# Three small reorderings in a fused attention and ternary-expert kernel on one core: two weight signs behind the first tanh, one value product behind a down product, one block's sums copied out of PSUM by ScalarE

## The chip, the core and the metric

The kernel runs on one NeuronCore of a Trainium2 chip. The core has five engines that run their own instruction streams and meet at semaphores: TensorE (PE in the profile) multiplies matrices into the accumulator memory PSUM; VectorE (DVE) and ScalarE (ACT) read and write PSUM and the on-chip memory SBUF; GpSimd (POOL) works on SBUF; SyncE (SP) issues the transfers to and from HBM. Weight loads of TensorE have a row of their own, PEld. Each engine takes its instructions in program order, so an instruction that waits holds up everything behind it on its engine.

The metric is the device time of one launch in microseconds, all data starting and ending in HBM. Of the kernel before, three timed executions are shown; their median is 1167.89 us.

## The reference, cut to what matters

The input is 2 x 2048 rows of 512 numbers. An attention over 64 fixed latent keys and a gated expert network follow one another, each with a normalisation before and after and a residual sum.

```python
# attention: 16 heads of 32, 64 latent keys per head, the four largest logits are kept
Q = (h @ Wq.T + bq)...;  V = (h @ Wv.T + bv)...
attn_logits = einsum('bhtd,lhd->bhtl', Q, latent) / sqrt(32)
topk_logits, topk_idx = top_k(attn_logits, 4)
weighted = einsum('bhtk,bhtkd->bhtd', softmax(topk_logits), latent_h[..., topk_idx])
attn_output = (weighted + V) @ Wo.T + bo

# expert network, 512 -> 2048 -> 512, weights rounded to -1, 0, 1 times a scale
wu, wg, wd = ternary_quant(W_up), ternary_quant(W_gate), ternary_quant(W_down)
hidden = silu(x @ wu.T) * (x @ wg.T)
ffn = hidden @ wd.T

x = x + layernorm(attention(layernorm(x)))
x = x + layernorm(ffn(layernorm(x)))
```

`ternary_quant` takes the mean of |W| as the scale, divides, rounds and clips to -1, 0 or 1.

## The kernel before, in words

The 4096 rows are worked in eight blocks (`NB`) of 512 rows; a block is four tiles of 128 rows. A block's expert network is sixteen chunks `e` of 128 hidden columns. The order of all instructions on all engines is the program's order: a manual schedule is in force and nothing is moved by a planner.

**First part.** A written list of steps, `FIRST_STEPS` (line 35 on), does block 0's attention, starts block 1's, and turns part of the expert weights into ternary form. A weight tile is made in three steps: `sum_abs` (ScalarE) for the scale, `rounded` (line 228, GpSimd, in place) and `sign` (line 232, ScalarE, raw to `tern`). The last four steps on the list are `rdd0 rdd1 sgd0 sgd1`: the rounding and the sign of the first two tiles of the down weights (`tern_d`). The tiles that the list does not make are made during block 0's experts by `rest(e, place)` (line 872) from the table `REST` (line 865): for the chunk that an entry names, the rounding is issued behind `tanh`, the sign behind `high`.

**The loop over chunks.** For each chunk e of a block (line 995 on), the order is: `up("u", e)`, eight matmuls into the PSUM buffer `pu`; `tanh` (ScalarE, L693); in block 0 `rest(e, "tanh")`; `silu` (VectorE, L696), which frees `pu`; `up("g", e)` into `pg`; `gate` (VectorE, L701), which frees `pg`; `high` (ScalarE, L712), a rounded copy of the product; in block 0 `rest(e, "high")`; `down(e - 1)`, the eight matmuls of the chunk before into the four accumulators `acc` (L727); `low` (VectorE, L717), what the rounded copy leaves over. `pu` and `pg` exist once each (`ps_up`, one buffer per tag), so the next chunk's up product waits for this chunk's silu, and its gate product for this chunk's gate. The four `acc` tiles (`ps_acc`, four buffers) are shared by all blocks.

**The next block's attention** lies between these steps. `pieces` (line 882) gives a table: `put(e, k, f, ...)` places a step of the next block in chunk e at one of four places, in the order of the code: 3 behind the up product, 0 behind tanh, 1 behind the gate product, 2 behind the down product. For block 1, the value product `v` (four matmul instructions of two passes, L435) and its attention part `y` (two more, L452, and the ScalarE copy `attnT`, L442) of column chunk 0 stand at place 1 of chunk 5, those of column chunk 1 at place 1 of chunk 7. They write one of the two PSUM buffers of `ps_at`, which the logit products `l` (L362) also use; those are emptied by ScalarE into `w` (L370). VectorE does the top four (`m`, `r`, lines 376 and 383), `n` the weights, `z` (L415) a transpose that goes through HBM into `wT`.

**The end of a block.** Its last down product is issued in chunk 0 of the next block. Behind it, `y_stats` (VectorE, L249 and L250) takes mean and variance of each `acc` tile and `y_rstd` (GpSimd, L256 to L259) the inverse deviation. In chunk 1, behind silu and ahead of the gate product, `y_out` (line 765) applies the norm to each of the four tiles: `Norm.apply` (line 275, L276, VectorE, out of PSUM into an SBUF `row` buffer, of which there are four), a GpSimd addition to the residual (L769) and the output transfer by SyncE (L771). The block's own first down product into `acc` is issued in chunk 1 and needs the four tiles free. The last block has no next attention in it.

Of the kernel before, what the change touches and what calls it, by code (L numbers as in the profile page):

```python
# [42 lines left out]
y3 scg rdg6 o3_2 yc3 rdg4 o2_3 sgg6 o3_3 ost2 rdg0 sgg4 o1_3 ost3 ors2 sgg0 o0_3 ost1 ors3 nq1  # L43
sd4 onm2 ost0 ors1 oap2 onm3 oap3 ors0 oad2 oad3 rdg2 onm0 fst2 oap0 nq2 nqc1 oad0 frs2 sgg2
onm1 fst3 oap1 fap2 frs3 oad1 fst1 nq3 nqc2 fap3 frs1 fst0 fap1 frs0 ftr3 fap0 nqc3 fhi3 ftr0
flo3 fhi0 flo0 ftr1 fhi1 ftr2 flo1 fhi2 flo2 totd scd rdd0 rdd1 sgd0 sgd1
"""

LAST_O = ((0, 3), (1, 3), (2, 3), (3, 3))
# [9 lines left out]
def latent_attention_ternary_glu(  # L59
# [15 lines left out]
    nc = tc.nc  # L75
    NT, D = x_in.shape
    E = wuT.shape[1]
    DC = D // P
# [3 lines left out]
    NB = NT // TB  # L82
# [49 lines left out]
    def load_x(b):  # L132
        x_tiles[b] = []
        for t in range(TT):
            xt = work.tile([P, D], F32, tag="x", name=f"x_{b}_{t}", bufs=2 * TT)
            r = b * TB + t * P
            nc.sync.dma_start(out=xt, in_=x_in[r : r + P, :])
            x_tiles[b].append(xt)
# [4 lines left out]
    def load_normed(b):  # L143
        for t in range(TT):
            xt = work.tile([P, D], F32, tag="xa", name=f"xa_{b}_{t}", bufs=TT)
            r = b * TB + t * P
            nc.sync.dma_start(out=xt, in_=x_in[r : r + P, :])
            normed[b, t] = xt
# [79 lines left out]
    def rounded(n, i):  # L228
        w = raw[n, i]
        nc.gpsimd.tensor_scalar(w, w, inverses[n], MAGIC, ALU.mult, ALU.add)  # L230

    def sign(n, i):
        j = i if n != "d" or i < 6 else 6 + (i - 6) // 2
        if (n, j) not in tern:
            tern[n, j] = wpool.tile([P, CH], F32R, tag="chunk", name=f"tern_{n}_{j}", bufs=6 * DC)
        q = tern[n, j] if j == i and i < 6 or n != "d" else tern[n, j][:, (i % 2) * D : (i % 2 + 1) * D]
        nc.scalar.activation(q, raw[n, i], AF.Sign, bias=minus_magic)  # L237
# [42 lines left out]
    def row(name):  # L280
        return work.tile([P, D], F32, tag="row", name=name, bufs=4)
# [250 lines left out]
    class FirstAttention(SecondAttention):  # L532
# [79 lines left out]
        def y_copy(self, c):  # L612
            nc.scalar.activation(
                self.attnT[:, c, :], self.pv.pop(c), AF.Identity, bias=bqv_sb[:, 1, c : c + 1]
            )
# [57 lines left out]
    class Experts:  # L673
# [58 lines left out]
        def y_stats(self, t):  # L732
            self.norm.stats(t, self.acc[t])

        def y_rstd(self, lo, hi):
            self.norm.rstd(lo, hi, out_scale)

# [26 lines left out]

        def y_out(self, t, engine=nc.gpsimd):
            x = x_tiles[self.b][t]
            y = row(f"y_{self.b}_{t}")
            self.norm.apply(y, self.acc[t], t)
            engine.tensor_tensor(x, x, y, ALU.add)  # L769
            r = self.b * TB + t * P  # L770
            nc.sync.dma_start(out=out[r : r + P, :], in_=x)  # L771
# [4 lines left out]
    A = FirstAttention(0)  # L776
# [83 lines left out]
    for step in FIRST_STEPS.split():  # L860
# [2 lines left out]


    REST = (
        [(1, "d", 2)] + [(2 + i // 2, "u", 2 * i + 1) for i in range(DC)]
        + [(4 + i // 2, "g", 2 * i + 1) for i in range(DC)]
        + [(6, "d", 3), (7, "d", 4), (8, "d", 5)]
        + [(9 + i // 2, "d", 6 + i) for i in range(DC)]
# [1 line left out]

    def rest(e, place):
        for chunk, n, i in REST:
            if chunk == e and place == "tanh":
                rounded(n, i)
            elif chunk == e and place == "high":
                sign(n, i)
# [4 lines left out]
    def pieces(A, after):  # L882

        at = {(e, k): [] for e in range(EC) for k in range(4)}

        def put(e, k, f, *args):
            at[e, k].append(lambda: f(*args))

        if A.b > 1:
            if A.b == 2:  # L890
                put(0, 0, A.a_apply, 0)
                put(0, 0, A.a_apply, 1)
                put(0, 1, A.a_trans, 0)
                put(0, 1, A.a_trans, 1)
                put(0, 1, A.a_apply, 2)
                put(0, 1, A.a_apply, 3)
                put(0, 2, A.a_trans, 2)
                put(0, 2, A.a_trans, 3)
            put(1, 0, A.q, 0)
            put(2, 0, A.q, 1)  # L900
            put(4, 0, A.q, 2)
            put(6, 0, A.q, 3)
        put(1, 1, A.l, 0)
        put(2, 2, A.l, 1)
        for i in range(8):
            put(2 + i, 0, A.m, i)
            put(2 + i, 2, A.r, i)
            put(3 + i, 3, A.e, i)
            put(3 + i, 1, A.n, i)
            put(3 + i, 1, A.z, i)  # L910
        for c in range(2):
            if A.b > 1:
                put(5 + 2 * c, 0, A.v, c, gate_psum)
                put(5 + 2 * c, 0, A.y, c)
            put(5 + 2 * c, 0, A.l, c + 2)
            if A.b == 1:
                put(5 + 2 * c, 1, A.v, c)
                put(5 + 2 * c, 1, A.y, c)
        for c in range(2, DC):
            put(5 + 2 * c, 1, A.v, c)  # L920
            put(5 + 2 * c, 1, A.y, c)
        if after is not None and after.b == 2:
            put(14, 2, after.a_stats, 0)
            put(14, 2, after.a_stats, 1)
            put(15, 1, after.a_stats, 2)
            put(15, 1, after.a_stats, 3)
            put(15, 1, after.a_rstd, 0, 4)
        elif after is not None:
            put(10, 2, after.a_stats, 0)
            put(10, 2, after.a_stats, 1)  # L930
            put(11, 0, after.a_stats, 2)
            put(11, 0, after.a_stats, 3)
            put(11, 0, after.a_rstd, 0, TT)
            for t in range(TT):
                put(11, 1, after.a_apply, t)
            for c in range(DC):
                put(11, 2, after.a_blocks, c)
            put(15, 2, after.a_load)
        put(11, 2, A.o, 0, range(DC), gate_psum)
        put(11, 2, A.o_bias, 0)  # L940
        for t in range(1, TT):
            put(11, 2, A.o, t)
            put(11, 2, A.o_bias, t)
        put(11, 2, A.o_rstd, 0, 2)
        put(12, 1, A.o_rstd, 2, 4)
        put(12, 2, A.o_apply, 0)
        put(12, 2, A.o_apply, 1)
        put(13, 0, A.o_apply, 2)
        put(13, 0, A.o_apply, 3)
        put(13, 1, A.f_stats, 0)  # L950
        put(13, 1, A.f_stats, 1)
        put(13, 1, A.f_rstd, 0, 2)
        put(13, 2, A.f_stats, 2)
        put(13, 2, A.f_stats, 3)
        put(13, 2, A.f_rstd, 2, 4)
        put(14, 0, A.f_apply, 0)
        put(14, 0, A.f_apply, 1)
        put(14, 1, A.f_alloc)
        put(14, 1, A.f_trans, 0)
        put(14, 1, A.f_trans, 1)  # L960
        put(14, 1, A.f_apply, 2)
        put(14, 1, A.f_apply, 3)
        put(15, 0, A.f_trans, 2)
        put(15, 0, A.f_trans, 3)
        return at

    prev = None
    for b in range(NB):
        if b > 0:
            A, nxt = nxt, after  # L970
        after = None
        F = Experts(b, (A.hi, A.lo))
        at = {}
        for e in range(EC):
            if e == 4 and 0 < b < NB - 1:
                load_x(b + 1)
            if e == (12 if b == 0 else 6) and b + 2 < NB:
                load_normed(b + 2)
            if e == 4:
                after = (SecondAttention if b == 0 else Attention)(b + 2) if b + 2 < NB else None  # L980
                if b + 1 < NB:
                    later = pieces(nxt, after)
                    at.update({k: v for k, v in later.items() if k[0] >= 4})
            elif e == 0 and b + 1 < NB:
                at.update({k: v for k, v in pieces(nxt, None).items() if k[0] < 4})

            def do(k):
                for f in at.get((e, k), ()):
                    f()

            def first(place):
                if b == 0:
                    rest(e, place)

            F.up("u", e)
            do(3)
            F.tanh(e)
            first("tanh")
            do(0)
            F.silu(e)  # L1000
            if e == 1 and prev is not None:
                for t in range(TT):
                    prev.y_out(t)
            F.up("g", e)
            do(1)
            F.gate(e)
            F.high(e)
            first("high")
            if b == NB - 1 and e >= EC - 2:
                pass  # L1010
            elif e > 0:
                F.down(e - 1)
            elif prev is not None:
                prev.down(EC - 1)
            do(2)
            if e == 0 and prev is not None:
                for t in range(TT):
                    prev.y_stats(t)
                prev.y_rstd(0, TT)
            F.low(e)  # L1020
        prev = F
# [73 lines left out]
```

## Time and profile before

| | before |
|---|---|
| timed executions, median (lowest to highest) | 1167.89 us (1167.62 to 1168.21) |
| profiled execution, its own time | 1165.54 us |
| span of the profiled execution, first to last instruction | 1163.7 us |
| mean granted clock of TensorE | 0.997 |
| PE busy | 1144.5 us, 98% |
| VectorE busy | 854.1 us, 73% |
| ScalarE busy | 370.8 us, 32% |
| GpSimd busy | 174.4 us, 15% |

The span is what the trace covers; the execution's own time is 1.8 us more. In the rows of a timeline the first number is the start in us from the span's start, the second the length, then engine, line of the program, operation, tile written and tiles read with their shape; in brackets at the end stands how long the engine was idle before it and what ended that. In a line of waits the numbers are total us, how many and the longest. In a table of stretches each engine has its busy us and, in brackets, its instructions; behind them stand the granted clock, the share of DMA time and GB/s.

### The profile page before, as it was taken

What the parts mean: (1) busy time and instruction counts of PE and PEld (TensorE: products, weight loads), DVE (VectorE), ACT (ScalarE), POOL (GpSimd) and SP (SyncE); (2) the same over time, 40 slices, a digit from 0 to 9 for tenths busy, and PEclk for the clock granted to TensorE, in tenths of its full rate; (3) what the DMA queues carried; (4) which work ended last, traced back from release to release, by engine and by line L of the source; (5) the groups of instructions that cost most, each with busy time, mean ns of one, the idle gap of its engine ahead of it and who ended that gap; (6) DMA issues with size and microseconds to landing.
All of it is one profiled execution on the core that took longest, in us unless ns stands there. A gap on an engine that the chain in (4) does not pass through costs nothing.

```text
span 1163.7 us, 14548 instructions
## 1 busy us (share of the span) xinstructions
PE 1144.5 (98%) x4730; PEld 786.2 (68%) x4730; DVE 854.1 (73%) x2974; ACT 370.8 (32%) x653; POOL 174.4 (15%) x213
## 2 busy tenths in 40 slices
PE   9999999999999999999999999999999999999997
PEld 5447665776757666677757766587665866757885
DVE  6977984967967779668887688776886868847335
ACT  4984531333213332123222232122331232312222
POOL 1056001310023000320003200032001320013001
PEclk9999999999999999999999999999999999999999
DMA  9700211023212221122220231211411112100000
GB/s 348 294 0 6 68 63 47 1 88 102 64 37 64 82 91 57 34 73 82 91 82 0 73 127 56 72 34 42 138 61 55 37 63 83 64 10 10 28 1 36
DMA packets 73323, 80.38 MB, mean 69 GB/s; under 512 B 7200, under 2 KB 46368, under 8 KB 73248
## 3 DMA queue, kind: packets, MB, share of 16 engines
q1 hardware_dynamic: 73248, 79.46, 20.9%
q8 instruction: 37, 0.61, 0.2%
q14 instruction: 38, 0.31, 0.1%
HBM read 51.12 MB, written 28.31 MB: 68 GB/s over the span
## 4 chain that ended last, share of the span: by engine, by line
PE 87%; DVE 4%; DMA 3%; ACT 2%; issue 1%; POOL 1%; SPq 1%; ACTq 0%; POOLq 0%
PE acc L727 19%; PE pg L684 19%; PE pu L684 19%; PE pv L435 8%; PE po L463 8%; PE pq L348 7%; PE pv L452 2%; PE pl L362 2%; PE pt_f L286 1%; DMA raw_d<-in_wdT 1%; DMA raw_g<-in_wgT 1%; DMA bo_sb<-in_bo 1%; DVE left L388 1%; DMA raw_u<-in_wuT 1%; ACT tern_g L237 1%
## 5 line engine op out<-in xcount | busy, mean ns | idle before, releaser
L684 PE MATMUL pg<-hT_f,tern_g 128*128 128x512 f32 x512 | 211.7, 413 | 0.0
L684 PE MATMUL pu<-hT_f,tern_u 128*128 128x512 f32 x512 | 204.4, 399 | 1.5 <-DVE h L696 1.5
L727 PE MATMUL acc<-tern_d,hi 128*128 128x512 f32 x512 | 203.8, 398 | 1.7 <-DVE y L276 1.7
L727 PE MATMUL acc<-tern_d,lo 128*128 128x512 f32 x512 | 200.3, 391 | 0.1
L684 PE MATMUL pu<-lT_f,tern_u 128*128 128x512 f32 x512 | 200.2, 391 | 0.1
L684 PE MATMUL pg<-lT_f,tern_g 128*128 128x512 f32 x512 | 199.8, 390 | 0.0
L712 ACT CAST hi<-h 128x512 fp32r<-128x512 f32 x128 | 79.4, 620 | 260.0 <-DVE h L701 259.9
L693 ACT ACTIVATE h<-pu,columns 128x512 f32<-128x512 f32 x128 | 87.2, 682 | 216.4 <-PE pu L684 215.6
L701 DVE TENSOR_TENSOR h<-h,pg 128x512 f32<-128x512 f32 x128 | 86.2, 673 | 78.7 <-PE pg L684 77.9
L696 DVE SCALAR_TENSOR_TENSOR h<-h,pu 128x512 f32<-128x512 f32 x128 | 86.2, 674 | 71.2 <-ACT h L693 71.2
L717 DVE TENSOR_TENSOR lo<-h,hi 128x512 fp32r<-128x512 f32 x128 | 96.2, 752 | 35.6 <-ACT hi L712 35.6
L727 PEld LDWEIGHTS acc<-tern_d,hi 128*128 128x128 f32 x512 | 96.2, 188 | 36.2 <-issue 15.0
L684 PEld LDWEIGHTS pg<-hT_f,tern_g 128*128 128x128 f32 x512 | 96.2, 188 | 26.2 <-issue 4.1
L684 PEld LDWEIGHTS pu<-hT_f,tern_u 128*128 128x128 f32 x512 | 96.6, 189 | 24.7 <-DVE h L696 2.4
L684 PEld LDWEIGHTS pg<-lT_f,tern_g 128*128 128x128 f32 x512 | 96.3, 188 | 24.2 <-issue 5.7
L684 PEld LDWEIGHTS pu<-lT_f,tern_u 128*128 128x128 f32 x512 | 96.7, 189 | 21.5 <-issue 1.7
L727 PEld LDWEIGHTS acc<-tern_d,lo 128*128 128x128 f32 x512 | 96.4, 188 | 19.7 <-DVE lo L717 0.9
L435 PE MATMUL pv<-hT,wv 128*128 128x512 f32 x224 | 100.9, 593 | 2.2 <-ACT w L370 2.1
L388 DVE MATCH_REPLACE8 left<-m,w 128x64 f32<-128x64 f32 x512 | 100.3, 210 | 0.0
L463 PE MATMUL po<-wo,attnT 128*128 128x512 f32 x224 | 97.3, 592 | 0.0
L348 PE MATMUL pq<-hT,wq 128*128 128x512 f32 x192 | 86.3, 592 | 0.0
L463 PEld LDWEIGHTS po<-wo,attnT 128*128 128x128 f32 x224 | 42.6, 190 | 50.7 <-issue 48.5
(128 smaller groups left out, 1321.4 us busy)
## 6 DMA issues: line engine op xcount, KB each, us to landing
dz<-z SPq DMA_DIRECT2D x56, 256.0 KB, 2.0
wT<-dz SPq DMA_DIRECT2D x224, 64.0 KB, 1.9
x<-in_x SPq DMA_DIRECT2D x32, 256.0 KB, 3.5
out_x<-x SPq DMA_DIRECT2D x31, 256.0 KB, 2.0
xa<-in_x SPq DMA_DIRECT2D x24, 256.0 KB, 3.4
da<-za SPq DMA_DIRECT2D x20, 256.0 KB, 2.9
hT<-da SPq DMA_DIRECT2D x20, 256.0 KB, 5.2
raw_u<-in_wuT SPq DMA_DIRECT2D x8, 512.0 KB, 8.6
```

The lines of the kernel that those rows point to most:

```text
L348: nc.tensor.matmul(pq, lhsT=wq[:, k, c * P : (c + 1) * P], rhs=self.taken(k), start=(k == 0), stop=(k == DC - 1),)
L362: nc.tensor.matmul(pls[pr][:, t * P : (t + 1) * P], lhsT=qT[rows, t * P : (t + 1) * P], rhs=lk[rows, c, :], start=True, stop=True, tile_po ...
L388: nc.vector.match_replace(left[:, g, :], m8[:, g, :], w[:, g, :], TAKEN)
L435: nc.tensor.matmul(self.pv[c], lhsT=wv[:, k, c * P : (c + 1) * P], rhs=self.ordered(k), start=(k == 0), stop=False,)
L463: nc.tensor.matmul(self.po[t], lhsT=self.attnT[:, c, t * P : (t + 1) * P], rhs=wo[:, c, :], start=(c == 0), stop=(c == DC - 1),)
L684: nc.tensor.matmul(p, lhsT=tern[n, 2 * k + e // 8][:, (e % 8) * P : (e % 8 + 1) * P], rhs=part[:, k, :], start=(k == 0 and i == 0), stop=( ...
L693: nc.scalar.activation(self.h[e], self.pu[e], AF.Tanh, scale=half_u[0])
L696: nc.vector.scalar_tensor_tensor(self.h[e], self.h[e], 1.0, self.pu.pop(e), ALU.add, ALU.mult)
L701: nc.vector.tensor_tensor(self.h[e], self.h[e], self.pg.pop(e), ALU.mult)
L712: nc.scalar.copy(hi, self.h[e])
L717: nc.vector.tensor_tensor(lo, self.h.pop(e), self.hid[e][0].bitcast(F32), ALU.subtract)
L727: nc.tensor.matmul(self.acc[t], lhsT=part[:, t * P : (t + 1) * P], rhs=wd, start=(e == 0 and i == 0), stop=(e == EC - 1 and i == 1),)
```

## The change

It has three parts.

1. The two signs of the first down-weight tiles leave the written list. Sign 0 is issued behind the tanh of chunk 0 of block 0, sign 1 behind its `high`. Their roundings stay where they were.
2. For block 1, the value product of column chunk 0 moves from place 1 of chunk 5 (ahead of the down product) to place 2 (behind it). Column chunk 1 stays.
3. In the last block (which ends the second to last), a ScalarE copy of each `acc` tile into an SBUF row is issued ahead of the statistics of that tile. The statistics still read `acc`; the apply of `y_out` reads the copy and writes it in place. The other blocks are as before.

```diff
-flo3 fhi0 flo0 ftr1 fhi1 ftr2 flo1 fhi2 flo2 totd scd rdd0 rdd1 sgd0 sgd1
+flo3 fhi0 flo0 ftr1 fhi1 ftr2 flo1 fhi2 flo2 totd scd rdd0 rdd1
...
+        def y_copy(self, t):
+            self.y = getattr(self, "y", {})
+            self.y[t] = row(f"y_{self.b}_{t}")
+            nc.scalar.copy(self.y[t], self.acc[t])
...
         def y_out(self, t, engine=nc.gpsimd):
             x = x_tiles[self.b][t]
-            y = row(f"y_{self.b}_{t}")
-            self.norm.apply(y, self.acc[t], t)
+            if self.b == NB - 2:
+                y = self.y[t]
+                self.norm.apply(y, y, t)
+            else:
+                y = row(f"y_{self.b}_{t}")
+                self.norm.apply(y, self.acc[t], t)
             engine.tensor_tensor(x, x, y, ALU.add)
...
-        [(1, "d", 2)] + [(2 + i // 2, "u", 2 * i + 1) for i in range(DC)]
+        [(0, "d", 0), (0, "d", 1), (1, "d", 2)] + [(2 + i // 2, "u", 2 * i + 1) for i in range(DC)]
...
         for chunk, n, i in REST:
-            if chunk == e and place == "tanh":
+            if e == 0:
+
+                if chunk == 0 and i == ("tanh", "high").index(place):
+                    sign(n, i)
+            elif chunk == e and place == "tanh":
                 rounded(n, i)
...
             if A.b == 1:
-                put(5 + 2 * c, 1, A.v, c)
-                put(5 + 2 * c, 1, A.y, c)
+                put(5 + 2 * c, 2 - c, A.v, c)
+                put(5 + 2 * c, 2 - c, A.y, c)
...
                 for t in range(TT):
+                    if b == NB - 1:
+                        prev.y_copy(t)
                     prev.y_stats(t)
```

## The prediction

> **What bounds the kernel now.** I read the page's busy shares first, then the waits of TensorE, then the timeline around each long wait, then the clock by stretch. TensorE (PE) is busy 98% of the span:
>
> ```profile
> PE 1144.5 (98%) x4730; PEld 786.2 (68%) x4730; DVE 854.1 (73%) x2974; ACT 370.8 (32%) x653; POOL 174.4 (15%) x213
> PE pv L435 <- ACT w L370: 2.1, 1, 2.1
> PE acc L727 <- DVE y L276: 1.7, 1, 1.7
> PE pu L684 <- DVE h L696: 1.5, 1, 1.5
> ```
>
> The last three lines are the longest waits of PE (total, how many, longest). Each happens once and all else is under 1.1 us, so only these three places can repay moving work on other engines. The first two places, both in block 0:
>
> ```profile
> 92.08 2.25 ACT L237 ACTIVATE tern_d<-raw_d,columns 128x1024 fp32r<-128x1024 f32 x2 [2.44 <-POOL raw_d L230]
> 94.24 0.67 ACT L693 ACTIVATE h<-pu,columns 128x512 f32<-128x512 f32 x1
> 95.68 0.50 PE L684 MATMUL pu<-hT_f,tern_u 128*128 128x512 f32 x1 [1.53 <-DVE h L696]
> ...
> 123.93 2.19 ACT L237 ACTIVATE tern_g<-raw_g,columns 128x1024 fp32r<-128x1024 f32 x2
> 125.67 0.69 DVE L717 TENSOR_TENSOR lo<-h,hi 128x512 fp32r<-128x512 f32 x1
> 127.23 1.07 ACT L370 ACTIVATE w<-pl 128x512 f32<-128x512 f32 x2
> 127.87 3.70 PE L435 MATMUL pv<-hT,wv 128*128 128x512 f32 x8 [2.13 <-ACT w L370]
> ```
>
> At 92 us two signs stand ahead of the first tanh on ScalarE; expert chunk 1's up product waits behind tanh and silu. At 125 us the value product waits until ScalarE has emptied one of two PSUM buffers. The third place, start of the last block, with the clock:
>
> ```profile
> 1072.20 2.97 DVE L276 TENSOR_SCALAR y<-acc,mv_y,rs_y 128x512 f32<-128x512 f32 x4 [1.02 <-POOL rs_y L259]
> 1073.16 0.47 PE L727 MATMUL acc<-tern_d,hi 128*128 128x512 f32 x1 [1.68 <-DVE y L276]
> 1075.09 0.68 DVE L701 TENSOR_TENSOR h<-h,pg 128x512 f32<-128x512 f32 x1
> ...
> 1075.00:1077.00 2.00, 2.00 (x6) 1.49 (x5) 1.32 (x3) 0.62 (x1) 2.00 (x3) 0.52 0.59 223
> 1077.00:1079.00 2.00, 2.00 (x7) 1.54 (x7) 0.42 (x1) 0.00 (x0) 1.55 (x1) 0.63 0.46 170
> ```
>
> In the two stretches the granted clock (third number from the end) falls to 0.52 and 0.63; matmuls step at 0.425 us instead of 0.2265 (eight in 1.81 us). So this wait costs far more than 1.7 us. Last, how the two engines that share work on the rows disturb each other, in an earlier place of block 7:
>
> ```profile
> 1043.67 1.52 POOL L479 TENSOR_TENSOR x<-x,o 128x512 f32<-128x512 f32 x1 [1.75 <-DVE o L276]
> 1043.96 1.78 DVE L717 TENSOR_TENSOR lo<-h,hi 128x512 fp32r<-128x512 f32 x1
> 1045.15 1.74 POOL L479 TENSOR_TENSOR x<-x,o 128x512 f32<-128x512 f32 x1
> 1045.67 1.51 DVE L276 TENSOR_SCALAR o<-o,mv_o,rs_o 128x512 f32<-128x512 f32 x1
> ```
>
> An apply that reads SBUF takes 0.54 us alone but 1.51 beside a POOL add, ending 0.29 us after that add does; the subtraction ends 0.55 us after its add. The 28 applies that read PSUM take 0.80 us each whether POOL adds or not.
>
> **Part 1, the signs.** Nothing is removed: the same two signs of 1.15 us move, and no DMA and no POOL work goes with them. The first up product ends at 92.32, so tanh runs 92.36 to 93.03, silu (0.69) to 93.75, and the second up product may start where PE is free: its last matmul began at 93.77, plus a step, 94.00. It started at 95.68, so 1.68 is gained here. Behind the tanh on ScalarE now stand sign 0 (to 94.10), the high part (gate ends 94.89, so to 95.54) and sign 1 (to 96.60); tanh 1 waits for sign 1 instead of for PE at 95.97, and silu 1 ends 97.95, where gate 1 may begin anyway (its matmuls end 97.8). Sign 0 is needed by the first down product at about 98.95. So late next is nothing up to chunk 2. From there to 127 us the chain runs through VectorE (DVE), which is busy 4.8 to 4.9 of each 5 us from 110 on and moves up as a whole, but meets POOL's roundings, which do not move (busy without a gap from 90.93 to 110.34). In the trace two operations of DVE lost 0.37 and 0.41 there (1.06 and 1.10 against 0.69). Coming 1.7 earlier they find more roundings left; a loss is at most one rounding of 0.81 each, and a third operation may be hit. I take 1.4 us; ends 0.7 and 1.7.
>
> **Part 2, the value product.** Six matmuls and one ScalarE copy move behind the down product of chunk 4; no DMA. In the times of before: PE is free at 125.58. The down product's first matmul can go, the second needs the low part (done 126.36), so it runs from 126.42 on and ends its eight steps at 128.00. The value product's PSUM buffer is empty at 127.80: no wait. So 2.29 of standstill becomes about 0.6, worth 1.7 at this point. What is queued behind: on ScalarE the copy of the values (it waited for PE until 132.65) stood ahead of high part 5 and two signs; now high part 5 runs at 131.08 behind its gate (131.04), the signs to 133.8, then the copy to 134.44, the exponentials to 135.1, tanh 6 to 135.72 instead of 137.16. So DVE's silu 6 starts 1.44 earlier, and with it everything up to the next two copies that empty PSUM; the second value product starts at 143.65 instead of 145.09, now 0.7 behind PE where it was 0.25. What DVE and ScalarE allow, 1.44, therefore decides. Behind 150 us the trace has no PE wait to the block's end and all shifts together. I take 1.4; ends 0 (the chain of DVE does not move at all) and 1.7.
>
> **Part 3, the copies.** Four copies PSUM to SBUF are added on ScalarE. No row has this form; the nearest is the copy of attention's 128x512 PSUM tile, 0.58 to 0.59 us, 0.5 when one follows another. The rows they write were last read by the transposes that ended at 1058.8. They start behind high part 0 (ends 1067.43), are done by 1069.5, and the tanh behind them began at 1069.77, when its matmuls ended: hidden. Were that cover gone (copies of 0.8, as DVE reads PSUM), tanh 1 would end 0.9 late, still before its silu blocks PE (1073.14). The PSUM sums are free when the statistics end, 1069.79, not when the applies do, so the down product runs at 1071.33 without a wait.
>
> Late next is the gate of chunk 1, which stands on DVE behind the four applies, and whose PSUM buffer PE needs for the gate product of chunk 2, now already at 1074.95. The applies read SBUF now. Following the rows above: apply 0 runs 1072.20 to 1072.74, apply 1 to 1073.20 (the second of a pair took 0.54 beside a waiting add), add 0 then holds until 1074.34, apply 2 ends 1074.63, add 1 holds until 1075.78, apply 3 ends 1076.07, the gate 1076.68. PE starts at 1076.73: 1.78 of new wait. The low part behind it is issued at 1077.37, meets the last add (until 1078.46) and ends 1079.0; the down product's second matmul wanted it at 1078.78: 0.27 more. Sum of the loss after the change 2.05. Before: that gate product began at 1079.13 against 1074.95, a loss of 4.18. Gain 2.1. SP's output DMAs follow the adds, which end at 1078.5 as before.
>
> The low end: every apply but the first costs 1.51 and the clock falls again. Of the 4.18, 1.62 is the half clock (from 1075.23 to 1078.66 eight steps took 3.43 instead of 1.81). 2.8 + 0.3 + 1.62 = 4.7, so 0.6 lost (three applies of 1.51, each overlapping the next by 0.08, end the gate about 1.0 later than above). The high end: applies of 0.54 throughout, gate done at 1075.1, loss nearly none: 4.1 gained.
>
> Two rules of the Trainium skill bear on this part. In "SBUF — State Buffer", section "Who interferes with whom", whoever of DVE and GpSimd issues first holds the shared pair of ports for its whole instruction, and an operation that reads one tensor from PSUM is exempt. It speaks against this change, and the 1.51 and 0.80 us rows agree with it; by the rule the gain is the 2.1 of the sum, by the row of a lone apply (0.54) it would be 4.1. "TensorE: Matmul & The Clock Gate", section "Part 1: The HAM clock gate", of the Trainium skill has the clock fall after an idle window of about 3.4 us; here it fell with no gap above 1.68 us, so the measurement decides and a fall after a 1.8 us gap is not excluded, as it would be by that page.
>
> **Sum.** 1.4 + 1.4 + 2.1 = 4.9 us off the profiled 1165.54 us (span 1163.7 and 1.8 around it), 1160.6 there. The timed median is 2.35 us above that execution, for reasons the profile does not show; taken off it, 1163.0 us.
>
> **The rivals.** (A) No turn-taking: all applies run at 0.54 us because DVE keeps winning over POOL. For it: two in a row did. Against it: the third operation at 1043.96 lost. Gain 4.1 in part 3: 1161.0 us. (B) The half clock is not what part 3 saves, either because it falls again behind the new 1.8 us wait or because the timed runs of before did not have it. For it: the fall at 1075 with gaps of 1.68 and three of about 0.4. Against it: after the gaps of 1.53 and 2.13 us in block 0 the clock stayed 1.00. Without the 1.62, part 3 gives 0.5: 1164.6 us. (C) Block 0 is bound by DVE and POOL, and the two gains there come to 0.6 together instead of 2.8, as new waits of PE at about 104 to 127. For it: DVE's 97%. Against it: DVE's own start hangs on the chain that moves. 1165.2 us. (D) Slower: the new wait in front of the gate product starts a longer spell at half clock. Each us of it costs 0.47 (0.425 against 0.2265 a step). It eats the 4.9 at 10 us and is beyond 0.2% at 15 us, where the spell of before lasted 3.2; a clock that stays down for 16 us gives 1170.5 us. Nothing in block 0 speaks for it.
>
> **How the numbers follow.** 0.2%, about what a measurement of this kernel can tell from no change, is 2.3 us: below 1165.6 is faster, above 1170.2 slower. Chances: the sum 0.52, A 0.12, B 0.18, C 0.12, D 0.06. The sum, A and most of B (0.14) are faster, of C half; what remains of B and C, and a little of the sum for terms all at their low ends, is no change: 0.81 faster, 0.14 same, 0.05 slower. The range leaves out D and the far ends of A and C: 1160.6 (A with parts 1 and 2 near their high ends) to 1166.4 (C with part 3 at 0.5 and little left of part 1). The sum's own range is 1162.0 to 1164.0.
>
> **What would show it.** Right: no wait of PE for the first silu, the second up product at about 94.0; no PE gap of 2 us ahead of a value product, high part 5 ahead of the value copy; the down product in the last block without a wait for the applies; a wait of some 1.8 us of the gate product on DVE's gate; applies of 0.54, 0.54, 1.5, 1.5 us. Wrong: clock below 1.00 in the last block; tanh 1 there later than its matmuls; PE waits on low parts or gates between 104 and 127 us that add up to more than 1 us.

## The result, and the profile after

The changed kernel takes 1164.45 us (median of seven executions, 1163.04 to 1166.71); the kernel before, in seven executions taken with them, 1167.62 us (1166.61 to 1168.42). The ratio is 0.9973 with a 95% interval of 0.9962 to 0.9985, so 3.2 us are gained by the medians, where 4.9 were forecast. The time lies in the range of 1160.6 to 1166.4 that was given, 1.45 us above the point. Single executions of one kernel scatter by more than that: of 61 executions of the kernel before, the extremes are 1164.35 and 1169.99 us. So traces, one execution each, are read below for places, and medians and ratios for amounts.

The busy line of the page of after. TensorE is as busy as before; the 4 instructions more on ScalarE are the copies:

```profile
PE 1144.4 (98%) x4730; PEld 785.2 (68%) x4730; DVE 855.1 (74%) x2974; ACT 372.7 (32%) x657; POOL 174.5 (15%) x213
```

TensorE's waits in after (total us, how many, longest):

```profile
PE pt_a L286 <- DVE h_a L276: 3.0, 2, 2.5
PE pg L684 <- DVE h L701: 2.4, 1, 2.4
...
PE acc L727 <- DVE lo L717: 0.6, 2, 0.5
...
PE pv L435 <- ACT w L370: 0.2, 1, 0.2
```

The three waits of before, 2.1, 1.7 and 1.5 us, are gone. One of 2.4 us is new: the gate product waits for VectorE's gate. The first line is at the launch's start, ahead of everything that the change touches; input landed late there, and by 91 us this execution ran 0.90 us behind that of before. That is taken off below where "net" is said.

Block 0 in the timeline of after:

```profile
93.30 0.69 ACT L693 ACTIVATE h<-pu,columns 128x512 f32<-128x512 f32 x1 [2.76 <-PE pu L684]
93.89 1.14 ACT L237 ACTIVATE tern_d<-raw_d,columns 128x1024 fp32r<-128x1024 f32 x1
94.85 0.41 PE L684 MATMUL pu<-hT_f,tern_u 128*128 128x512 f32 x1
...
130.15 0.62 ACT L712 CAST hi<-h 128x512 fp32r<-128x512 f32 x1 [2.77 <-DVE h L701]
130.67 2.19 ACT L237 ACTIVATE tern_g<-raw_g,columns 128x1024 fp32r<-128x1024 f32 x2
132.76 0.67 ACT L442 ACTIVATE attnT<-pv,bqv_sb 128x512 f32<-128x512 f32 x1
...
142.58 3.70 PE L435 MATMUL pv<-hT,wv 128*128 128x512 f32 x8 [0.16 <-ACT w L370]
```

Tanh runs ahead of the sign, and the second up product starts at 94.85 without a wait (before: 95.68, after 1.53 of wait). The copy of the values, `attnT`, runs behind the high part and the two signs. The second value product starts at 142.58 where it started at 145.09: 2.51 earlier, 3.4 net.

The last block in the timeline of after, and then the clock there in stretches of 2 us (granted clock third from the end):

```profile
1064.54 0.69 DVE L701 TENSOR_TENSOR h<-h,pg 128x512 f32<-128x512 f32 x1 [0.34 <-PE pg L684]
...
1065.26 0.62 ACT L712 CAST hi<-h 128x512 fp32r<-128x512 f32 x1 [1.78 <-DVE h L701]
...
1065.78 2.04 ACT L739 COPY y<-acc 128x512 f32<-128x512 f32 x4
...
1066.39 0.70 DVE L249 BATCH_NORM_STATS2 st_y<-acc 128x6 f32<-128x512 f32 x1 [1.17 <-ACT y L739]
...
1070.34 0.50 PE L727 MATMUL acc<-tern_d,lo 128*128 128x512 f32 x1 [0.17 <-DVE lo L717]
...
1071.91 3.84 DVE L276 TENSOR_SCALAR y<-y,mv_y,rs_y 128x512 f32<-128x512 f32 x4 [1.03 <-POOL rs_y L259]
1072.54 5.58 POOL L779 TENSOR_TENSOR x<-x,y 128x512 f32<-128x512 f32 x4 [0.67 <-DVE y L276]
...
1075.67 0.67 DVE L701 TENSOR_TENSOR h<-h,pg 128x512 f32<-128x512 f32 x1
...
1076.40 0.50 PE L684 MATMUL pg<-hT_f,tern_g 128*128 128x512 f32 x1 [2.37 <-DVE h L701]
```

```profile
1074.00:1076.00 2.00, 0.03 (x1) 0.00 (x0) 2.00 (x3) 0.00 (x0) 2.00 (x3) 1.00 0.35 131
1076.00:1078.00 2.00, 1.60 (x5) 1.32 (x6) 1.31 (x2) 1.21 (x2) 2.00 (x2) 0.76 0.48 181
1078.00:1080.00 2.00, 2.00 (x6) 1.52 (x6) 1.58 (x3) 0.00 (x0) 0.12 (x1) 0.50 0.56 212
```

The down product no longer waits for the applies, as meant. But the statistics were held up for 1.17 us, and what held them is the copy, the other reader of the same sums, which itself stands on ScalarE behind the high part of chunk 0. In the kernel before they followed the gate at once, as two rows of VectorE there show:

```profile
1066.08 0.69 DVE L701 TENSOR_TENSOR h<-h,pg 128x512 f32<-128x512 f32 x1 [0.34 <-PE pg L684]
1066.69 0.69 DVE L249 BATCH_NORM_STATS2 st_y<-acc 128x6 f32<-128x512 f32 x1
```

From gate to statistics 0.61 us then, 1.85 now: everything behind them on VectorE, up to the gate that TensorE waits for, is 1.24 late. TensorE meets this delay twice. The down product waits for its low part, which stands behind the statistics, and takes 2.28 us instead of 1.81, so 0.47 are lost; the gate product of chunk 2 then starts 2.53 us behind its place (2.37 of them idle). And behind the new wait the clock falls to half, as it did behind the old one.

One measure serves for all runs below: from the start of chunk 1's gate product to that of chunk 3's up product in the last block are five products of eight matmuls, 40 steps, 9.06 us at 0.2265 us a step. What a trace takes beyond that is called the loss of the place below. Before: 1069.51 to 1082.78, a loss of 4.2 us. After: 1067.96 to 1081.78, a loss of 4.8. So in the profiled execution part 3 cost 0.6 us, and the whole gain came from block 0.

### The profile page after: what moved, and what is told of

It is laid out like the page before. It is cut to its first block, busy times and chain, and to the rows that moved or that the text cites. A ratio compares the mean times of both kernels' runs of the same rounds, so it can differ in the third digit from the quotient of the medians.

```text
span 1162.8 us, 14556 instructions
## 1 busy us (share of the span) xinstructions
PE 1144.4 (98%) x4730; PEld 785.2 (68%) x4730; DVE 855.1 (74%) x2974; ACT 372.7 (32%) x657; POOL 174.5 (15%) x213
## 4 chain that ended last, share of the span: by engine, by line
PE 88%; DVE 4%; DMA 3%; ACT 2%; SPq 1%; POOL 1%; issue 1%; ACTq 0%; POOLq 0%
PE pg L684 19%; PE pu L684 19%; PE acc L727 19%; PE po L463 8%; PE pv L435 8%; PE pq L348 7%; PE pv L452 3%; PE pl L362 2%; PE pt_f L286 1%; DMA raw_d<-in_wdT 1%; PE pq L557 1%; DMA raw_g<-in_wgT 1%; DMA bo_sb<-in_bo 1%; DVE left L388 1%; DMA raw_u<-in_wuT 1%; ACT junk L206 1%
## 5 line engine op out<-in xcount | busy, mean ns | idle before, releaser
L717 DVE TENSOR_TENSOR lo<-h,hi 128x512 fp32r<-128x512 f32 x128 | 99.1, 774 | 35.1 <-ACT hi L712 35.1
```

What stands on the lines that cost most here:

```text
L717: nc.vector.tensor_tensor(lo, self.h.pop(e), self.hid[e][0].bitcast(F32), ALU.subtract)
```

## The experiments

Times are medians; the kernel before ran beside each of three groups, at 1167.06, 1166.96 and 1167.12 us, the third group on another chip, so runs of different groups are compared by their ratios to it. The numbers in square brackets behind a ratio are its 95% interval. A stretch at half clock is called a spell. Theories at the start: the gain is that of block 0 alone, and part 3 gives nothing because its statistics wait for the copies and the applies stand ahead of the gate; the rival is that part 3 gives what was forecast and block 0 fell short.

### Parts 1 and 2 without the copies, and the copies alone

The first kernel is the changed one with

```diff
-                    if b == NB - 1:
-                        prev.y_copy(t)
...
-            if self.b == NB - 2:
+            if False:
                 y = self.y[t]
```

> The changed kernel without its copies (parts 1 and 2 alone; the last block as before). Theory 1, from the two traces: block 0 gives 3.4 us (the second value product starts 2.51 us earlier in a run whose first 90 us were 0.90 us late) and part 3 gives nothing. Then 3.4 us below the kernel before, as fast as the changed kernel or a little faster, with the 1.7 us wait of the last block's first down product and its half clock back. Theory 2, the sum on record: part 3 gives about 2 and block 0 the rest of the 3.2 measured: 1.1 us below before.

The second is the kernel before with nothing but these lines and the apply out of the copy.

> Part 3 alone: copies in the last block, signs and value product as before. Theory 1: in the trace the four chunks' matmuls behind the first down product lose 4.75 us against 4.19 before, so 0.6 us slower than before, or equal. Theory 2: 2.1 us faster.

Measured: parts 1 and 2, 1164.27 us (nine executions), ratio 0.9972 [0.9961, 0.9983]; the copies alone, 1168.28 us (eleven), ratio 1.0010 [0.9999, 1.0021]. The changed kernel has 0.9973. So parts 1 and 2 are the whole gain and the copies add nothing; alone they lean to a loss (1.2 us by the medians), and the 2.1 us forecast for them lies outside the interval.

In the trace of the copies alone the same wait of 2.36 us stands ahead of the gate product, and the clock fell in two places, one of them in block 0 behind the old 2.1 us wait, where the trace of before had kept it at 1.00. The value product there takes 5.40 us instead of 3.70:

```profile
128.22 5.40 PE L435 MATMUL pv<-hT,wv 128*128 128x512 f32 x8 [2.12 <-ACT w L370]
```

```profile
129.00:132.00 3.00, 3.00 (x5) 1.25 (x4) 2.93 (x12) 0.00 (x0) 0.00 (x0) 0.53 0.10 38
```

And in the trace of parts 1 and 2 the last block has the wait of before, 1.7 us, and no fall, but one at 93 us (two stretches of that trace):

```profile
93.00:96.00 3.00, 2.91 (x7) 2.13 (x7) 1.92 (x6) 0.00 (x0) 2.10 (x2) 0.51 0.04 8
...
1074.00:1077.00 3.00, 1.51 (x5) 0.77 (x6) 2.47 (x4) 0.00 (x0) 1.97 (x4) 1.00 0.00 0
```

So the half clock is not tied to one wait. The loss in the last block is 2.7 us there without it, against 4.2 in the trace of before with it. This 1.7 us wait stands in five traces of this record: three have the fall behind it (before and, of the runs below, part 2 alone and part 1 with unread matmuls; losses of 4.1 to 4.2) and two have not (this one, and part 1 alone; 2.7 each). So 1.5 us of what part 3 was to save is not always there to be saved.

### The statistics ahead of the copies

Only the order of the two readers of a tile changes:

```diff
                 for t in range(TT):
-                    if b == NB - 1:
-                        prev.y_copy(t)
                     prev.y_stats(t)
+                    if b == NB - 1:
+                        prev.y_copy(t)
```

> The changed kernel with each copy issued behind the statistics of its tile instead of ahead. Theory 1: the statistics wait for the copies only because of the order (they read the same tile and the copy comes first in the program), so they start right behind the gate of chunk 0 again, 1.2 us earlier, and the new wait of PE on the gate of chunk 1 falls from 2.4 to some 1.8 or below; the time falls by 0.6 us (wait alone) to 2.5 us (if the clock then stays at 1.00) against the changed kernel. Theory 2: copy and statistics disturb each other in any order, or the tanh behind the copies becomes late: no gain, and a tanh of chunk 1 later than its matmuls.

Measured: 1161.56 us (five), ratio 0.9956 [0.9943, 0.9969]. VectorE, ScalarE and TensorE in its last block:

```profile
1064.43 0.69 DVE L701 TENSOR_TENSOR h<-h,pg 128x512 f32<-128x512 f32 x1 [0.34 <-PE pg L684]
...
1065.04 0.69 DVE L249 BATCH_NORM_STATS2 st_y<-acc 128x6 f32<-128x512 f32 x1
...
1066.62 0.59 ACT L739 COPY y<-acc 128x512 f32<-128x512 f32 x1 [0.21 <-DVE st_y L249]
...
1070.55 3.85 DVE L276 TENSOR_SCALAR y<-y,mv_y,rs_y 128x512 f32<-128x512 f32 x4 [0.44 <-POOL rs_y L259]
...
1074.32 0.67 DVE L701 TENSOR_TENSOR h<-h,pg 128x512 f32<-128x512 f32 x1
...
1075.05 0.50 PE L684 MATMUL pg<-hT_f,tern_g 128*128 128x512 f32 x1 [1.59 <-DVE h L701]
```

The statistics follow the gate by 0.61 us again, and now each copy waits for the statistics of its tile (0.21 for the second). The reader that comes second in the program waits, whichever it is. The gate product waits 1.59 us instead of 2.37 and starts 1.76 behind its place, where the forecast had 1.78; the loss of the place is 2.2 us against the forecast's 2.05. The tanh of chunk 1 now comes late behind the copies, and silu waits 0.51 us for it, but TensorE does not wait for that silu. The clock stayed at 1.00 there in this execution. By the ratios this kernel is 1.7 thousandths below the changed one, with overlapping intervals; in the traces the loss fell by 2.6 us. The four rows of the apply are unchanged (3.85 us), so what remains is theirs.

### What the applies cost, and where they stand

In the first kernel the applies and additions of the last block move behind the low part of chunk 1, so that the gate no longer stands behind them:

```diff
-            if e == 1 and prev is not None:
+            if e == 1 and prev is not None and b < NB - 1:
...
             F.low(e)
+            if e == 1 and b == NB - 1:
+                for t in range(TT):
+                    prev.y_out(t)
```

> The changed kernel with the last block's four applies (and additions and transfers) issued behind the low part of chunk 1 instead of ahead of its gate; the copies have freed the accumulators, so nothing of the block needs the applies early. Theory 1: what part 3 lost is the gate standing behind the applies; without it PE waits for at most 0.3 us at the start of the last block, the clock stays at 1.00 there, and the kernel is about 4.4 us faster than the changed one, 7.5 below before. Theory 2: the applies delay the silu of chunk 2 instead, and PE waits 2 us there; within 1 us of the changed kernel.

In the second they stay, but VectorE does the four additions, one chunk later; the output transfers go with them:

```diff
                 self.norm.apply(y, self.acc[t], t)
+            if self.b == NB - 2:
+                return
             engine.tensor_tensor(x, x, y, ALU.add)
...
+        def y_add(self, t):
+            x = x_tiles[self.b][t]
+            nc.vector.tensor_tensor(x, x, self.y[t], ALU.add)
...
             F.low(e)
+            if e == 2 and b == NB - 1:
+                for t in range(TT):
+                    prev.y_add(t)
```

> The changed kernel with the last block's four additions done by VectorE behind chunk 2 instead of by GpSimd beside the applies. Theory 1: the applies then take 0.54 us each, 2.0 in all instead of 3.8; the gate of chunk 1 ends 1.8 us earlier and PE's wait of 2.4 us on it is 0.5 to 0.7: 1.8 us below the changed kernel, 3.4 where a spell of half clock goes too. Theory 2: applies in place from SBUF take 1.5 us for another reason, and the wait stays 2.4.

The third has both mends, the statistics first and the applies late.

> Both mends together: copies behind the statistics, applies behind the low part of chunk 1. Theory 1: as the run with late applies, less the 0.3 to 0.5 us by which its first down product waited for the low part: 1160.0 us, 7 below before. Theory 2: the copies then keep the tanh of chunk 1 back and PE waits on its silu: slower than the run with late applies.

Measured: applies behind the gate 1160.51 us (six), 0.9949 [0.9933, 0.9965], loss of the place 0.5 us; additions on VectorE 1161.62 us (five), 0.9952 [0.9940, 0.9963], loss 1.2; both mends 1159.26 us (five), 0.9934 [0.9922, 0.9947], loss 0.0. With the additions on VectorE the four applies, and the gate product behind them, read:

```profile
1071.80 1.92 DVE L276 TENSOR_SCALAR y<-y,mv_y,rs_y 128x512 f32<-128x512 f32 x4 [1.03 <-POOL rs_y L259]
...
1074.37 0.50 PE L684 MATMUL pg<-hT_f,tern_g 128*128 128x512 f32 x1 [0.45 <-DVE h L701]
```

1.92 us for four, where beside GpSimd's additions they took 3.84 (0.54, 0.54, 1.5 and 1.5). So the turn-taking of the two engines, in which each is held up while the other runs, is shown by its removal, and it alone was worth 1.9 us on VectorE. With the applies behind the gate the loss of the place fell by 4.3 us in the trace, near the 4.4 expected, but by the ratios the time fell by 2.8: a sum taken from one trace with a spell was again more than the timed executions gave. Late statistics and slow applies are two causes; the place they share is the gate behind them.

### Part 1 alone and part 2 alone

Part 1: `sgd0 sgd1` leave the list, the value product and the copies as before. Part 2: only `put(5 + 2 * c, 2 - c, ...)`.

> Part 1 alone (the two signs behind the first tanh). Theory 1, from the traces: the second up product starts 1.6 us earlier, DVE's work at 110 us 2.0 us earlier, and the wait of the value product at 126 us stays 2.1. So about 1.8 us below the kernel before, a little more where the removed wait had brought a spell of half clock (1.6 us each) in some executions. Theory 2: the gain is lost to POOL's roundings before 127 us: under 0.7 us.

> Part 2 alone (the value product behind the down product). Theory 1: the second value product starts 1.4 to 1.6 us earlier against the first up product than before, the wait of 2.1 us is 0.4 on the low part; 1.5 us below the kernel before, more where the removed wait had brought a spell of half clock. Theory 2: DVE's chain does not move and gives the 1.7 us back as waits by 145 us: no change.

Measured: part 2, 1165.11 us (eight), ratio 0.9980 [0.9970, 0.9991], 1.9 us by the medians; in its trace the second value product starts 1.6 us earlier, counted from the first up product. Part 1, 1167.34 us (twelve), ratio 0.9998 [0.9987, 1.0009]: no gain. Yet its trace shows one: the second up product starts at 94.81, and the first value product at 126.88 instead of 127.87, in an execution that like that of after was 0.9 late from the start. Each execution's mean clock is on record, and the difference goes with it. Eight of part 1's twelve executions had 0.995 or less, against 5 of the 20 of the kernel before beside them. Its fastest, the profiled one, had 0.998 and took 1163.49 us. The five executions at 0.995 to 0.998 lie 1.7 to 2.4 us below the mean of those of the 61 of the kernel before with the same clock; the seven at 0.994 do not (1168.06 on average against 1168.17). So part 1 seems to gain its time and lose it again in more spells of half clock, which the mean clock alone does not prove. Traces place such a spell between 90 and 97 us, behind the first part's transposes, in five of the nine kernels that hold part 1 and have no unread matmuls there (parts 1 and 2 above is one), not in the profiled execution of part 1 itself, and in none of the three without part 1. Where the spells of the eight slower-clocked executions lie no trace shows.

The reading was tested by keeping TensorE busy there: part 1 alone with six unread matmuls of an idle weight tile among the transposes of the first part (steps `wm1` and `wm2`; they write a spare PSUM tile, the output is not touched).

```diff
-... frs0 ftr3 fap0 nqc3 fhi3 ftr0
-flo3 fhi0 flo0 ftr1 fhi1 ftr2 flo1 ...
+... frs0 ftr3 wm1 fap0 nqc3 fhi3 ftr0
+wm2 flo3 fhi0 flo0 ftr1 wm1 fhi1 ftr2 wm2 flo1 ...
```

> Part 1 alone, with six matmuls that nobody reads among the transposes just ahead of the first up product (85 to 92 us), where PE stands for 0.2 to 0.6 us at a time. Theory 1: part 1's 1.6 us are real and are eaten in many executions by a spell of half clock that starts behind the transposes (four of seven traces of kernels with part 1 show one between 90 and 96 us); with PE busier there, spells become rarer and the time is 1 to 2 us below that of part 1 alone. Theory 2: part 1 gives nothing, spell or no spell, or the spells stay: within 0.7 us of part 1 alone.

Measured: 1164.65 us (twelve), ratio 0.9977 [0.9966, 0.9988], 2.1 thousandths or 2.5 us below part 1 alone, though it does more work. One of its twelve executions had a clock of 0.995 or less. The stretch of 93 to 96 us in its trace:

```profile
93.00:96.00 3.00, 3.00 (x15) 2.38 (x14) 1.72 (x3) 2.24 (x4) 3.00 (x4) 1.00 0.00 0
```

That agrees with the reading that half clock ate part 1's gain; the two intervals just touch. The unread matmuls were not tried in the kernel before, so how much of the 2.5 us they would give without part 1 is open.

### Does the clock fall because TensorE stands still?

The changed kernel, with eleven unread matmuls ahead of chunk 2's gate product in the last block, so that TensorE does not stand still in the new wait:

```diff
+            if b == NB - 1 and e == 2:
+                spare = at_psum("spare")
+                for i in range(11):
+                    nc.tensor.matmul(
+                        spare, lhsT=tern["d", 0][:, :P], rhs=F.parts[0][:, 0, :], start=True, stop=True
+                    )
             F.up("g", e)
```

> The changed kernel with eleven matmuls that nobody reads (into a free PSUM buffer) in PE's wait on the gate of chunk 1 in the last block; they take 11 x 0.2265 = 2.5 us of a wait of 2.5. Theory 1: the half clock behind this wait comes from the standstill; with PE busy it stays at 1.00, and the time falls by up to 1.6 us against the changed kernel, by less where the changed kernel's executions had no spell there. Theory 2: the clock falls for another reason: it falls again, and the time is the same or some tenths more.

Measured: 1163.78 us (ten), ratio 0.9971 [0.9961, 0.9981]. Its trace, a timeline and a stretch:

```profile
1073.59 2.65 PE L1021 MATMUL spare<-hT_f,tern_d 128*128 128x512 f32 x11
1076.13 0.50 PE L684 MATMUL pg<-hT_f,tern_g 128*128 128x512 f32 x1
```

```profile
1076.00:1079.00 3.00, 3.00 (x13) 2.08 (x12) 2.31 (x3) 1.21 (x2) 1.88 (x2) 1.00 0.55 208
```

The clock stays at 1.00 and the loss of the place is 3.5 us instead of 4.8. In the timing the difference to the changed kernel is 0.2 thousandths, within the intervals. The 2.4 us wait has the fall behind it in both traces that hold it, those of after and of the copies alone. So in the traces the fall goes with the standstill, but one execution without a fall is weak evidence where the 1.7 us wait goes without one in two traces of five. How many of the timed executions of the changed kernel have the fall is not settled by this run: a fall in half of them would be lost in the scatter.

### A version that beats both

In the trace of after some of the 2.5 us gained in block 0 is lost again in later blocks (0.5 by 695 us, 0.3 each by 835 and 975). SyncE's queue at the first of these places (timeline of after):

```profile
674.89 1.85 SPq L137 DMA_DIRECT2D x<-in_x  x4
678.74 0.33 SPq L420 DMA_DIRECT2D dz<-z  x1
681.92 1.75 SPq L423 DMA_DIRECT2D wT<-dz  x4
```

From the issue of the write to HBM (`dz`) to that of the read back (`wT`), which needs the write landed, 3.2 us pass behind four loads of 256 KB. With both mends, the loads are issued at chunk 5 instead of 4:

```diff
-            if e == 4 and 0 < b < NB - 1:
+            if e == 5 and 0 < b < NB - 1:
                 load_x(b + 1)
```

> Both mends, and the next block's x rows loaded from chunk 5 on instead of chunk 4, behind the transfers that the value product waits for. In the traces the value product of chunk 5 waits for 0 to 0.66 us in some of the blocks when the x loads stand ahead of its transfer. Theory 1: these waits go, about 1 us below the kernel with both mends. Theory 2: the wait moves to the next transfer, no difference.

Measured: 1158.85 us (six), ratio 0.9922 [0.9908, 0.9936], the lowest of all, 8.3 us below the kernel before by the medians and 9.1 by the ratio. In its queue the read back is issued 2.1 us after the write:

```profile
679.48 0.34 SPq L420 DMA_DIRECT2D dz<-z  x1
681.54 1.73 SPq L423 DMA_DIRECT2D wT<-dz  x4
683.31 1.87 SPq L137 DMA_DIRECT2D x<-in_x  x4
```

Against both mends alone (0.9934) the gain is 1.2 thousandths with overlapping intervals; the trace shows the mechanism, the timing does not prove the amount. From the middle of block 3 to the start of the last block the lead over the trace of before goes from 2.0 us to 2.3 here, and from 2.0 to 0.2 in the trace of both mends.

The same with unread matmuls in the first part, as in part 1 kept busy:

> Both mends, with the six unread matmuls among the transposes ahead of the first up product. Theory 1 as for part 1 with them: 0.5 to 1.5 us below the kernel with both mends, no spell between 90 and 96 us. Theory 2: the unread matmuls delay the transposes by what they save.

Measured: 1159.74 us (six), 0.9937 [0.9924, 0.9950]: no gain, although its trace has no fall at 90 to 96 us. It has one at 11 to 18 us instead. Keeping TensorE busy went with a gain for part 1 alone and with none here. None of the five executions of both mends had a clock of 0.995 or less, against eight of twelve of part 1 alone, so there was less to save; why the two differ in that stays open.

## Why the prediction was right in direction and 1.5 us short

**Part 1 (1.4 us, ends 0.7 and 1.7).** The mechanism holds step by step: no wait for the first silu, and the second up product at 94.85, which is the forecast's 94.00 plus the 0.90 of late start, within 0.05. VectorE does move up through GpSimd's roundings: in the trace of part 1 the first value product starts 0.99 earlier, 1.9 net. The 0.3 us taken off for these roundings were not lost: net of the late start VectorE is 1.85 us ahead at 105 us and 1.86 at 127. The step also read the row of before short: besides its two operations the low part at 102.36 was held up, 1.65 us against 0.69, and that 0.96 is more than the 0.81 given as the most that one can lose. What the step left out is the clock. Timed alone the part gave 0.0 (0.9987 to 1.0009); with the unread matmuls it gave 2.7 by the ratio, which may hold a share of their own.

**Part 2 (1.4 us, ends 0 and 1.7).** Timed 1.9 by the medians, with 1.4 inside the interval of 1.1 to 3.5. High part 5 and the signs run ahead of the value copy as written. The two parts together were put at 2.8; timed 2.8 by the medians (3.3 by the ratio), in the trace 3.4, which is the 1.9 of part 1's trace and the 1.6 of part 2's. Rival C, block 0 bound by VectorE and GpSimd, is out.

**Part 3 (2.1 us, ends -0.6 and 4.1).** This is the step that failed, and in it one sentence: "The PSUM sums are free when the statistics end, 1069.79". It kept the statistics at their time of before, as if copies and statistics read the same sums side by side, and put the wait of one reader for the other at nothing. The copies were indeed hidden from tanh, but the statistics waited for them and came 1.24 us late, and so did the chain behind, which is the one priced: the down product lost 0.47 us on its low part and the gate product came 2.53 us behind its place instead of 1.78. The clock then fell again, the first of the signs named for being wrong. The low end had 0.6 us lost and the trace has 0.6, but that match is luck: the low end priced three slow applies, of which there were two, and not late statistics. It is the case of rival B, half clock not saved, for which 1164.6 us stood against the measured 1164.45, and that is partly luck too: B's fall came behind a longer wait than B had, its 0.5 us for part 3 was not seen, and block 0 gave 3.3 by the ratio where B had 2.8. Put back in order, the forecast's working is right: with the statistics first the loss is 2.2 against 2.05, and the applies of 0.54, 0.54, 1.5, 1.5 us ahead of the gate came as written.

**The other error** lies in the value put on the saving: the 4.18 us of before was read from one execution, and 1.5 of it was a fall of the clock that two of the five traces with the same wait do not show. A saving of half clock should have been weighted by how often it occurs.

**Rivals.** A, no turn-taking, is out: the second pair of applies lost to the additions. D, a long spell at half clock, is out: the fall in the last block lasted 3.4 us in both traces with the new wait, as in that of before.

## What to carry to other kernels

A copy that frees a buffer early is a second reader of it, and in this program the later of two readers waits for the earlier: issue the reader with the longer chain behind it first. When the wait of the bounding engine goes, look at what stands on the other engines' queues between the freed point and the next instruction it needs; here four applies that nobody was waiting for stood ahead of a gate that TensorE was waiting for, and moving them behind it was worth 2.8 us by the ratios where the copies alone gave nothing. Where a saving contains lost clock, take it from several executions, not from one trace.

## What the runs showed of the hardware that was not expected

The granted clock fell to half behind standstills of 1.7 to 2.4 us, and not in every execution: the same 1.7 us wait has the fall in the trace of before (0.50 from 1076 to 1078) and none in those of part 1 and of parts 1 and 2 (1.00). A spell also comes between 90 and 97 us behind transposes with gaps of 0.2 to 0.6 us (0.51 from 93 to 96 in the trace of parts 1 and 2). The eleven falls of these two kinds, in ten traces, have one length, whatever stood ahead of them: read in stretches of 1 us each lacks 1.7 us of clock, as 3.4 us at 0.50 do, and costs 1.5 to 1.6 us of time. What decides which standstill is followed by it was not found.

VectorE's applies that read and write SBUF beside GpSimd's additions took 3.84 us for four; without these additions, 1.92. The form that reads PSUM had taken 2.97 us for four in the same company, in the row of before, so the copy out of PSUM made these instructions 0.9 us slower in all.
